# Attention scores as two extra columns per head of the feature weights, in the set-up of a graph-attention kernel

## The chip, the cores and the metric

The kernel runs on one core of a Trainium2 chip. The metric is device time in microseconds, the median of the runs of one program. A core has a matrix engine (TensorE, PE in the profile; its weight loads are PEld), VectorE (DVE), ScalarE (ACT), GpSimd (POOL) and SyncE (SP). Engines run their own instruction queues in order and wait for each other by semaphores. Sixteen DMA engines move data; here SP, POOL and at the very start ACT ask for transfers. Matmul results go to PSUM, 8 banks of 128 x 512 float32 values.

## The reference

Two layers over 4096 nodes with 512 features and a dense 4096 x 4096 adjacency matrix. Layer 0 is graph attention with 8 heads of 64 features, layer 1 an attention inside 32 graphs. The change concerns layer 0 alone, and of it the first three lines:

```python
feats = jnp.einsum('nf,hfo->hno', X, W)                  # 8 heads, 4096 x 64 each
s_self = jnp.einsum('hno,ho->hn', feats, a_self)         # one score per node and head
s_neigh = jnp.einsum('hno,ho->hn', feats, a_neigh)
dense = s_self[:, :, None] + s_neigh[:, None, :]
dense = jnp.where(dense > 0, dense, ALPHA * dense)       # ALPHA = 0.2
dense = dense * A[None, :, :]
attn = jax.nn.softmax(dense, axis=-1)
out = jnp.einsum('hij,hjo->hio', attn, feats) + b[:, None, :]
```

Then a relu, a residual and a layer norm; layer 1 follows on the result.

Because a score is feats times a vector, it is also X times (W a): one column of 512 weights per head and kind of score.

## The kernel before

**Set-up** (lines 601 to 822). The 4096 nodes are 32 tiles of 128, taken in 8 blocks k of 4 tiles u. For each block:

- `load_rows(k)` (L617) asks on SP for four tiles of x, into four buffers `xt_f`.
- `turn_rows(k)` transposes them on PE (L661), 16 transposes of 128 x 128, four to each of four PSUM tiles `ps_set`; ACT copies each PSUM tile to `xT_f` (L664) and sums it on the way.
- `scores(k)` multiplies xT by `wa`, the 16 columns W a (L672), one 32-row strip of PSUM for each of the four chunks c of the 512 features; ACT copies the strips to `st` (L680).
- `exponentials(k)` multiplies `st` by `stack`, which adds the four strips and turns the scores to columns (L686), and takes five exponentials on ACT (L695 to L700): `e_all`, `d_all` and `pu_j`. DVE then splits `e_all` into bf16 parts (L703 to L717).
- `features(k, u)` multiplies one tile by W (L743): four matmuls of 512 columns into one PSUM tile, and DVE adds b into `fb` (L751).
- `scaled_features(k, u)` makes `gst` = fb times an exponential (DVE, L757) and `fst`, the features split into two rounded parts (ACT L765, DVE L766); POOL stores both to DRAM as `g_d` and `f_d` (L778). `gst`, `fst` and `fb` have three buffers each.
- `rows_of_exponentials(k)` transposes `pu_j` on PE (L722), ACT copies it (L726), POOL stores it to `pu_d` (L730). `columns_of_exponentials(k)` transposes the copy back (L735) into `pu_all` (DVE, L736).

After blocks 3, 4 and 5 POOL also loads a first part of the adjacency matrix (L596). At the end column sums of the features are formed (L576, L583).

The weights' score columns come from DVE at the very start: four chunks times two kinds, a product (L647) and a reduction (L650).

All PSUM tiles of the set-up come from one pool of seven banks, in turn; the eighth bank is `ps_misc`, which the adjacency transposes (L1122) use later.

**After the set-up** come four passes over the adjacency matrix, one per pair of heads. The first turns adjacency tiles (PE L1122), casts them on ACT (L1126) and stores them (`at_d`, POOL L1127); all passes run the matmuls L1381, L1401 and L1415 over them, with the comparisons L1361 (DVE) and L1370 (ACT). Layer 1 (L961 to L1103) runs in the last pass and after it. SP loads `p_row` and `u_row` from `pu_d` for the passes (L1306, L1309).

**The order of the work.** PE's instructions run in the order in which the program is written (`manual_schedule` for PE, L455). The other engines' queues are ordered by a planner, which takes what it holds to be ready, earlier program lines first; on the chip each queue then runs strictly in that order.

## Time and profile before

| what | value |
|---|---|
| median of 3 runs | 2079.16 us (2077.47 to 2079.18) |
| span of the profiled execution | 2080.8 us |
| PE, DVE, ACT, POOL busy, share of the span | 98%, 80%, 74%, 12% |
| set-up: first L1122 transposes of the first pass start at | 162.90 us |
| set-up: features of the last tile end at | 161.83 us |
| one block of the set-up (L686 of one block to that of the next) | 18.47 us |
| L743, 256 records of 128x512 | 116.9 us busy |
| L672 and L686, 64 records each | 9.6 and 8.1 us busy |
| f_d stores, 32 of 512 KB each | 7.7 us to land, median |

A page of the profile gives shares over the whole span. A fp32 matmul appears as two records. Records of pipelined matmuls overlap, so their busy time is longer than the distance between them; the distances stand in the chain, which follows the work that ended last back from the end. In the timeline, the brackets name what an instruction waited for. The profiled execution has no time of its own beside its span; it lies 1.6 us above the median.

### The profile page before, as it was taken

What the parts mean: (1) busy time and instruction counts of PE and PEld (TensorE: products, weight loads), DVE (VectorE), ACT (ScalarE), POOL (GpSimd) and SP (SyncE); (2) the same over time, 40 slices, a digit from 0 to 9 for tenths busy, and PEclk for the clock granted to TensorE, in tenths of its full rate; (3) what the DMA queues carried; (4) which work ended last, traced back from release to release, by engine and by line L of the source; (5) the groups of instructions that cost most, each with busy time, mean ns of one, the idle gap of its engine ahead of it and who ended that gap; (6) DMA issues with size and microseconds to landing.
All of it is one profiled execution on the core that took longest, in us unless ns stands there. A gap on an engine that the chain in (4) does not pass through costs nothing.

```text
span 2080.8 us, 38068 instructions
## 1 busy us (share of the span) xinstructions
PE 2045.7 (98%) x14982; PEld 1005.3 (48%) x14982; DVE 1660.4 (80%) x2040; ACT 1536.7 (74%) x1821; POOL 246.4 (12%) x393
## 2 busy tenths in 40 slices
PE   8999999999999999999999999999999999999997
PEld 4555555454445544444445444444454444445443
DVE  5557887878799998798999999999975984886654
ACT  3338888888878989788899889998885666567420
POOL 2343222222100000000000000000200210210111
PEclk9999999999999999999999999999999999999999
DMA  8999999999899999888999999989974764775211
GB/s 249 267 257 247 270 292 259 296 260 285 261 326 342 347 346 337 275 303 285 323 317 334 310 344 331 330 288 363 321 242 138 247 250 129 227 272 167 72 48 43
DMA packets 207881, 551.28 MB, mean 265 GB/s; under 512 B 25292, under 2 KB 66252, under 8 KB 207692
## 3 DMA queue, kind: packets, MB, share of 16 engines
q1 hardware_dynamic: 140748, 425.79, 59.0%
q0 software_dynamic: 62784, 121.91, 23.3%
q8 instruction: 120, 1.97, 0.4%
q10 hardware_dynamic: 4160, 1.05, 0.2%
q14 instruction: 69, 0.57, 0.1%
HBM read 491.79 MB, written 107.22 MB: 288 GB/s over the span
## 4 chain that ended last, share of the span: by engine, by line
PE 83%; DMA 7%; issue 4%; DVE 2%; ACT 2%; POOL 1%; SPq 0%; POOLq 0%; ACTq 0%; DVEq 0%
PE acc L1401 36%; PE accf L1381 20%; PE ps_set L743 5%; PE ps_m L1059 5%; DMA at_d<-at 5%; PE ps_m L987 5%; PE dens L1415 5%; PE ps_m L1014 1%; PE ps_m L1073 1%; ACT mark L1370 1%; DVE q L1361 1%; PE ps_m L1122 1%; PE ps_m L916 1%; DMA f_s<-f_d 1%; DMA hs_d<-hst 1%
## 5 line engine op out<-in xcount | busy, mean ns | idle before, releaser
L1361 DVE SCALAR_TENSOR_TENSOR q<-p_row,d_all,at 128x1024 f32<-128x1024 f32 x1024 | 1242.0, 1278 | 171.4 <-PE acc L1401 143.7
L1370 ACT ACTIVATE mark<-q,nb_all 128x1024 fp8e4<-128x1024 f32 x896 | 994.6, 1145 | 176.1 <-DVE q L1361 160.3
L1401 PE MATMUL acc<-q,g_s 128*32 128x512 f32 x8192 | 903.0, 593 | 1.1 <-DVE q L1361 0.4
L1401 PEld LDWEIGHTS acc<-q,g_s 128*32 128x32 f32 x8192 | 264.5, 110 | 594.1 <-issue 533.1
L1381 PE MATMUL accf<-at,f_s 128*128 128x512 f32 x2048 | 494.5, 397 | 2.3 <-issue 1.8
L1381 PEld LDWEIGHTS accf<-at,f_s 128*128 128x128 f32 x2048 | 379.9, 189 | 111.7 <-issue 29.1
L1141 ACT ACTIVATE ck<-ck,neg_half_f 128x1024 f32<-128x1024 f32 x128 | 146.0, 1140 | 20.5 <-DMA ck<-in_adj_dram 20.5
L1142 ACT ACTIVATE ck<-ck,neg_quarter 128x1024 f32<-128x1024 f32 x128 | 146.3, 1143 | 1.8
L1126 ACT CAST at<-ps_m 128x1024 fp32r<-128x1024 fp8e4 x128 | 120.2, 1025 | 12.3 <-issue 5.9
L1415 PE MATMUL dens<-mark,e_b 128*6 128x512 fp8e4 x2048 | 125.4, 379 | 2.7 <-ACT mark L1370 2.7
L743 PE MATMUL ps_set<-w_sb_f,xT_f 128*128 128x512 f32 x256 | 116.9, 605 | 0.1
L987 PE MATMUL ps_m<-x1T,M_sb 128*128 128x512 f32 x256 | 113.1, 595 | 1.6 <-ACT x1T L968 1.6
L1059 PE MATMUL ps_m<-wvT,x1T 128*128 128x512 f32 x256 | 114.2, 594 | 0.0
L1246 POOL DMA_DIRECT2D hs_d<-hst x12 | 10.7, 895 | 832.9 <-DVE hst L1236 739.0
L1366 DVE TENSOR_SCALAR mark<-q,d_all 128x1024 fp8e4<-128x1024 f32 x128 | 95.7, 748 | 4.8
L1415 PEld LDWEIGHTS <-e_b 128*6 128x6 bf16 x2048 | 52.7, 86 | 83.0 <-issue 38.8
L1127 POOL DMA_DIRECT2D at_d<-at x128 | 68.8, 538 | 178.0 <-ACT at L1126 111.0
L765 ACT ACTIVATE fst<-fb 128x512 fp32r<-128x512 f32 x32 | 20.3, 636 | 85.3 <-DVE fb L751 48.3
L987 PEld LDWEIGHTS ps_m<-x1T,M_sb 128*128 128x128 f32 x256 | 47.9, 190 | 63.1 <-issue 60.1
L1059 PEld LDWEIGHTS ps_m<-wvT,x1T 128*128 128x128 f32 x256 | 47.6, 190 | 57.2 <-issue 56.0
L743 PEld LDWEIGHTS ps_set<-w_sb_f,xT_f 128*128 128x128 f32 x256 | 49.0, 199 | 51.3 <-issue 49.9
L994 ACT ACTIVATE zT<-ps_m,zb 128x512 f32<-128x512 f32 x32 | 21.8, 683 | 70.3 <-PE ps_m L987 70.3
(185 smaller groups left out, 1119.2 us busy)
## 6 DMA issues: line engine op xcount, KB each, us to landing
at<-at_d SPq DMA_DIRECT2D x384, 512.0 KB, 6.0
ck<-in_adj_dram SPq DMA_DIRECT2D x128, 512.0 KB, 5.5
f_s<-f_d SPq DMA_DIRECT2D x128, 512.0 KB, 7.4
at_d<-at POOLq DMA_DIRECT2D x128, 512.0 KB, 14.8
g_s<-g_d SPq DMA_DIRECT2D x128, 256.0 KB, 5.6
f_d<-fst POOLq DMA_DIRECT2D x32, 512.0 KB, 7.7
p_row<-pu_d SPq DMA_DIRECT2D x32, 512.0 KB, 6.7
a_b<-in_adj_dram POOLq DMA_DIRECT2D x32, 512.0 KB, 16.8
```

The costliest lines, as they stand in the source:

```text
L743: nc.tensor.matmul(pf, tile_j(xTs[k][:, c].rearrange("p u n -> p (u n)"), u), w_sb[:, c, :], start=(c == 0), stop=(c == FC - 1),)
L987: nc.tensor.matmul(pz, L1["M"][:, f, ts(c, P)], x1T[:, f, :], start=(f == 0), stop=(f == FC - 1),)
L1059: nc.tensor.matmul(pv, x1T[:, f, ts(u, P)], L1["wvT"][:, f, :], start=(f == 0), stop=(f == FC - 1),)
L1126: nc.scalar.copy(at, both[:, :, k])
L1141: tc.keep_in_program_order(nc.scalar.activation(ck, ck, AF.Square, bias=neg_half))
L1142: nc.scalar.activation(ck, ck, AF.Abs, bias=neg_quarter, accum_out=binp[:, k : k + 1])
L1361: nc.vector.scalar_tensor_tensor(q, p_row[h], d_j, ats[r, c, j].bitcast(F32), op0=OP.max, op1=OP.mult)
L1366: nc.vector.tensor_scalar(mark, q, d_j, None, op0=OP.is_gt, saturate=False)
L1370: nc.scalar.activation(mark, q, AF.Sigmoid, bias=nb_all[:, j, hh : hh + 1], scale=BIG, saturate=False,)
L1381: nc.tensor.matmul(accf[:, s, :], f_s[j // 4][:, j % 4, w, :], ats[r, c, j][:, ts(s, HB)], start=(j == 0 and w == 0), stop=(j == NT - 1 an ...
L1401: nc.tensor.matmul(acc[o : o + 32, s, :], g_s[j // 4][:, j % 4, h, o % FH : o % FH + 32], qs[j, h][:, ts(s, HB)], start=(j == 0), stop=(j ...
L1415: nc.tensor.matmul(dens[lo : lo + 6, :], e_b[:, j, 2 * r + h, :], marks[j, h][:, ts(s, HB)], start=(j == 0), stop=(j == NT - 1),)
```

## The change

`wa`, `stack`, `scores` and the strip copies `st` go. The weights become 66 columns per head: 64 of W and two of W a, which DVE's reductions write into the same tile `w_sb`. A tile's features and scores come out of the same accumulation. 8 x 66 = 528 columns don't fit a PSUM bank, so each chunk is two matmuls of 264 columns into two banks, from a pool `ps_feat` with two such tiles; the other pool has three banks in place of seven. The scores of a tile are then multiplied by the factors of the exponents (`powers`, DVE) and exponentiated, tile by tile. In block 0 the features take 64 columns per head, and `first_scores` makes the scores of its four tiles with matmuls of 16 columns. The order within a block changes: the turning of the next block stands behind features (k, 0) in every block, rows and columns of the exponentials are formed one block later, and in the last block behind the loop. `fb` moves to the pool of `q` (six buffers), `prod` to that of `gst`.

```diff
-    ) as xtp, tc.tile_pool(name="ps_setup", bufs=7, space=PSUM) as pss:
+    ) as xtp, tc.tile_pool(name="ps_setup", bufs=3, space=PSUM) as pss, tc.tile_pool(
+        name="ps_feat", bufs=2, space=PSUM
+    ) as psf:
...
+        FW = FH + 2
+        w_sb = one.tile([P, FC, H, FW], F32, name="w_sb_f")
...
-        wa = one.tile([P, FC, 32], F32, name="wa")
-        nc.vector.memset(wa, 0.0)
         for c in range(FC):
             for k in range(2):
-                prod = three.tile([P, H, FH], F32, name="fb")
...
+                prod = three.tile([P, H, FH], F32, name="gst")
+                nc.vector.tensor_mul(prod, w_sb[:, c, :, :FH], a_b2[:, k])
+                nc.vector.tensor_reduce(w_sb[:, c, :, FH + k], prod, AX.X, OP.add)
+        powers = one.tile([P, 5, H], F32, name="powers")
+        for i, v in enumerate((ALPHA, 1.0, ALPHA - 1.0, 1.0 - ALPHA, -ALPHA)):
+            nc.vector.memset(powers[:, i, :], v)
...
                 if u == 0:
-                    pts[c] = pss.tile([P, 4, P], F32, name="ps_set")
+                    last = k == 0 and c == FC - 1
+                    pts[c] = misc([P, 4, P]) if last else pss.tile([P, 4, P], F32, name="ps_set")
...
-        def scores(k):
...
-        def exponentials(k):
...
+        def exponentials(k, u, sc):
+
+            j = 4 * k + u
+            if u == 0:
+                pu_js[k] = two.tile([P, 4, 2, H], F32, name="pu_j")
+            st = small.tile([P, 5, H], F32, name="st")
+            for lo, hi, w in ((0, 3, 1), (3, 5, 0)):
+                nc.vector.tensor_tensor(
+                    st[:, lo:hi].rearrange("p k (q h) -> p k q h", q=2),
+                    sc[:, None, :, :, w].to_broadcast([P, hi - lo, 2, H // 2]),
+                    powers[:, lo:hi].rearrange("p k (q h) -> p k q h", q=2),
+                    OP.mult,
+                )
+            nc.scalar.activation(e_all[:, j], st[:, 0:2], AF.Exp)
+            nc.scalar.activation(pu_js[k][:, u], st[:, 3:5], AF.Exp)
+            nc.scalar.activation(d_all[:, j, :], st[:, 2], AF.Exp)
...
         def features(k, u):
-            pf = pss.tile([P, H * FH], F32, name="ps_set")
+            pf = psf.tile([P, 2, HB], F32, name="ps_fe")
+            pf = pf[:, :, : H * FW // 2].rearrange("p q (h w) -> p q h w", w=FW)
+            cols = slice(0, FW if k else FH)
             for c in range(FC):
...
+                for q in range(2):
+                    nc.tensor.matmul(
+                        pf[:, q, :, cols],
+                        tile_j(xTs[k][:, c].rearrange("p u n -> p (u n)"), u),
+                        w_sb[:, c, 4 * q : 4 * q + 4, cols],
+                        start=(c == 0),
+                        stop=(c == FC - 1),
+                    )
+            fb = qp.tile([P, C], F32, name="q")[:, : H * FH]
...
+            if k:
+                exponentials(k, u, pf[:, :, :, FH:])
             return fb
+
+        def first_scores():
+
+            ps = pss.tile([P, 4, H, 2], F32, name="ps_set")
+            for u in range(4):
+                for c in range(FC):
+                    nc.tensor.matmul(
+                        ps[:, u],
+                        tile_j(xTs[0][:, c].rearrange("p u n -> p (u n)"), u),
+                        w_sb[:, c, :, FH:],
+                        start=(u == 0 and c == 0),
+                        stop=(c == FC - 1),
+                        skip_group_check=True,
+                    )
+            for u in range(4):
+                exponentials(0, u, ps[:, u].rearrange("p (q h) w -> p q h w", q=2))
...
         for k in range(NB):
             if k + 1 < NB:
                 load_rows(k + 1)
...
+            fbs = {}
+            for u in range(4):
+                fbs[u] = features(k, u)
+                if u == 0 and k + 1 < NB:
+                    turn_rows(k + 1)
+                if u == 1 and k:
+                    rows_of_exponentials(k - 1)
+                if u == 2 and k:
+                    columns_of_exponentials(k - 1)
+                if u == 2 and k == 0:
+                    first_scores()
+                    for v in range(3):
+                        scaled_features(k, v, fbs[v])
+                if k or u == 3:
+                    scaled_features(k, u, fbs[u])
...
+            parts_of_exponentials(k)
             if k in (3, 4, 5):
                 tc.keep_in_program_order(load_adjacency(0, 4 * (k - 3)))
+        rows_of_exponentials(NB - 1)
         pS = pss.tile([P, PR], F32, name="ps_set")
         sums_to_columns(pS, S_part)
...
```

`parts_of_exponentials(k)` holds the splitting into bf16 parts that stood at the end of `exponentials(k)`; the partial column sums (L804 to L812) now stand behind features (7, 0) and (7, 1). The last `columns_of_exponentials` stays where it was, behind the column sums.

## The prediction

> **What bounds the kernel now.** I read the page first (share of each engine, the chain), then a table by stage, then the chain inside the set-up, then its waits.
>
> ```profile
> span 2080.8 us, 38068 instructions
> PE 2045.7 (98%) x14982; PEld 1005.3 (48%) x14982; DVE 1660.4 (80%) x2040; ACT 1536.7 (74%) x1821; POOL 246.4 (12%) x393
> PE 83%; DMA 7%; issue 4%; DVE 2%; ACT 2%; POOL 1%; SPq 0%; POOLq 0%; ACTq 0%; DVEq 0%
> ```
>
> TensorE carries 83% of the chain. The change touches the set-up only, so the stage table decides (columns: stretch, length, busy us and count of PE, PEld, DVE, ACT, POOL, clock, DMA share, GB/s).
>
> ```profile
> 0.00:20.00 20.00, 14.17 (x38) 6.81 (x38) 10.82 (x31) 3.70 (x9) 0.81 (x10) 1.00 0.84 249
> 80.00:100.00 20.00, 20.00 (x80) 10.26 (x79) 10.95 (x27) 6.41 (x20) 8.07 (x11) 1.00 0.86 247
> 120.00:140.00 20.00, 20.00 (x80) 9.99 (x82) 11.01 (x28) 6.28 (x20) 8.97 (x12) 1.00 1.05 220
> 163.00:168.60 5.60, 2.46 (x32) 2.09 (x32) 4.42 (x7) 5.05 (x7) 3.63 (x6) 0.83 0.58 203
> ```
>
> From 20 to 163 us PE has no idle time; DVE and ACT are about half and a third busy; DMA is near full from 95 us on. One block of four tiles, as the chain shows it (start, length, what):
>
> ```profile
> 74.53 0.84 PE ps_set L686 x8
> 75.37 1.79 PE ps_set L661 x16
> 77.17 3.44 PE ps_set L743 x8
> 80.61 0.35 PE ps_set L735 x4
> 80.95 3.64 PE ps_set L743 x8
> 84.59 1.00 PE ps_set L672 x8
> 85.59 0.54 PE ps_set L722 x4
> 86.12 6.88 PE ps_set L743 x16
> 93.00 0.84 PE ps_set L686 x8
> ```
>
> The period is 93.00 - 74.53 = 18.47 us, all PE: 13.96 features, 1.79 transposes of x, 0.54 + 0.35 transposes of the exponentials, and 1.84 for what the change removes (L672 1.00, L686 0.84).
>
> Last, waits that cost PE nothing yet, and the end of the set-up:
>
> ```profile
> 112.27 0.69 DVE L757 TENSOR_TENSOR gst<-fb,e_all 128x512 f32<-128x512 f32 x1 [3.50 <-DMA g_d<-gst]
> 113.73 0.63 ACT L765 ACTIVATE fst<-fb 128x512 fp32r<-128x512 f32 x1 [8.23 <-DMA f_d<-fst]
> 114.65 0.63 ACT L664 ACTIVATE xT_f<-ps_set 128x512 f32<-128x512 f32 x1
> 162.90 1.33 PE L1122 MATMUL ps_m<-ident_b,a_b 128*128 128x128 bf16 x16
> 168.64 9.85 PE L1381 MATMUL accf<-at,f_s 128*128 128x512 f32 x32
> ```
>
> ACT stands at fst (L765) until an earlier f_d store lands, and behind it in ACT's queue stand the copies of the turned rows (L664). PE runs on only because seven PSUM tiles let it.
>
> **The change part by part** (against the profiled execution; its span of 2080.8 is 1.6 us, 0.08%, above the median 2079.16 of the runs, so I subtract the shift from the median).
>
> *Features.* Each fp32 matmul is two records. A 512-column record takes 3.43/8 = 0.429 us (L743, L1059), a 128-column one 0.112 (L661: 1.79/16; L1014: 3.57/32), both with a 128x128 weight load hidden. A line through both gives 0.224 us at 264 columns. A tile becomes 16 such records, 3.59 us, against 3.44: four tiles cost 0.61 more. Bounds: 0.220 (pure streaming at the slope 0.827 ns per column plus 2 ns) to 0.231 (adding the 17 ns by which L1381's 512-column single-pass record, 7.38/32 = 0.231, exceeds half of 0.429): 0.4 to 1.0 per block. The Trainium skill (Perfetto Trace Analysis, Matmuls) says larger matmuls are more efficient than smaller ones, which speaks against the split; by the two rows above that is 3 ns per record (0.2176 on the line at 256 columns against 0.429/2), inside the 0.61; the page gives no figure of its own for the sum.
>
> *Scores and stacking removed.* 1.00 + 0.84 off PE per block; also ACT's st copy (0.57) and a DVE memset and reduction (0.17, 0.25), both in the shade of PE. New period: 4 x 3.59 + 0.2 for changes of kind (13.96 - 8 x 4 x 0.429) + 1.79 + 0.54 + 0.35 = 17.23, so 1.23 less.
>
> *Exponentials per tile.* Per block eight small DVE products (nearest: L703, 0.18) and twelve exps (L695: 0.20, every 0.08) in place of five. At most 1.5 and 2.4 us on engines that have 9 and 13 us of every 20 free: nothing while PE is the limit. Chain per tile on DVE and ACT: 0.69 (fb) + 0.3 + 0.3 (exps) + 0.69 (gst) + 0.69 (stt) = 2.7 us, under the 3.6 of a tile, so two feature buffers suffice as long as no store is late.
>
> *Block 0.* Features (0,0) end at 14.75 as before. Next in PE's order is now the turning of block 1, whose rows are requested at 10.59 and land at about 18.2 (the DMA rate falls to nothing there); before, it ran at 21.79 and didn't wait. From 18.2: turning 1.97, features (0,1), (0,2) 7.05, first scores (32 records at 0.105, the rate of L686, 3.45), features (0,3) 3.6, features (1,0) 3.6: turning of block 2 at 37.9, against 38.44. But PE stands idle for 3.4 us. In the trace, after 3.04 idle us at the end of the set-up (1.82 + 1.22), the next 32 accf matmuls took 9.61 us instead of 7.38: the window's clock is 0.83 for that reason. So between 0 and 2.2 us for a cold clock; the idle stretch is like that row and I take 2.2: +1.7 in all. The skill (TensorE: Matmul & The Clock Gate, What's actually happening) has half rate after an idle window of some 3.4 us and full rate after as much work; by that page an estimate of 1.7 us in place of 2.2, and a sum of -0.9 in place of the -0.4 below.
> The product-and-reduce pairs now write into w_sb beside what features (0,u) read. If that were tracked by whole tiles, features (0,0) would end near 21.6, and block 2 be turned 1 us later than I take; but DVE already interleaves writes and reads of different elements of e_b (L710 twice before L711), so I leave that at 0.
>
> *Blocks 1 to 6.* From the turning of block 2 to the end of features (7,0): 148.40 - 38.44 = 109.96 before, 6 x 17.23 = 103.4 after: -6.6.
>
> *Block 7.* 161.83 - 148.40 = 13.43 before; 3 x 3.59 + 0.25 + 0.54 + 0.35 + 1.0 (partial sums) = 12.9 after: -0.5.
>
> *The tail.* rows_of_exponentials moves from before features (k,3) to one block later, for the last block behind everything. What moves: 4 transposes, an ACT copy (0.61), a POOL store pu_d (0.53 of issue), which passes the g_d and f_d stores of the next tiles on POOL; on SP the p_row and u_row loads (55.23, 56.10) wait a block longer, with the x rows behind them, which are needed only a block after they are asked for: nothing. But after the last features PE now waits for fb 0.8, products 0.3, exps 0.3 to 0.9 (fst may stand first on ACT), then 0.54 transposes, 0.80 column sums beside the ACT copy, 0.35: 3.4 us to the first L1122, against 1.07: +2.3 (1.5 to 3.5). Behind it wait the adjacency casts on ACT, then accf. One fst (0.54) no longer stands between the first casts: -0.5.
>
> *PSUM.* The turning needs four tiles and has three (one bank each), so chunk 3 waits for ACT's copy of chunk 0. Transposing starts at 0; chunk 0 is ready at 0.65, copied at 1.25, released at about 1.4; chunk 3 would start at 1.35. If ACT is free: 0.1 per block, +0.6 (0 to 4.2, see rivals).
>
> *Late stores.* With three banks ACT's wait reaches PE. Features (4,3) end at 108.03, so its fst was ready at 108.9 and ran 4.8 late. After, the first adjacency load and all behind it move up by 4.4 us, the features by 5: late by 5.3. Chunk 3 is released fst 0.55, copy 0.6 and 0.15 after that start, 7.5 us after features (4,3), and is due after 3.59 + 1.35 = 4.95: 2.6 us of PE idle. The later late stores (131.20, 148.12: 3.8 and 2.3 late) then fall under the 2.7 that is tolerated. Bounds: 0 (covered) to 5 (each of them felt): +2.6.
>
> Sum: +1.7 - 6.6 - 0.5 + 2.3 - 0.5 + 0.6 + 2.6 = -0.4 us. After the set-up PE is the limit, and the shift passes through: 2079.16 - 0.4 = 2078.8. I call 0.2% (4.2 us) the least that a measurement of this kernel tells from no change; this lies inside.
>
> **The rivals.**
> *A, the saving comes through (24%).* No cold clock, and the late stores stay hidden: -0.4 - 2.2 - 2.6 = -5.2, 2074.0. For it: no idle of 1.34 us at 19.5 slowed PE, and DMA share is only 0.65 and 0.50 in the last 10 us of the set-up, so stores are not the limit overall. Against it: the two rows used above.
> *B, ACT takes the exponentials before the first copy (22%); slower.* The exps of tile (k,0) need fb and two products, ready 1.15 us after its features. If ACT's order has them ahead of the copy of chunk 0, that ends near 2.0, chunk 3 starts at 2.1: 0.7 per block, 4.2 instead of 0.6; and in block 5 the exps wait for a DVE that waits for the late fst: 2 more. -0.4 + 3.6 + 2.0 = +5.2: 2084.4. It decides from a first copy that starts later than 0.75 us after the transposes. For it: today the exps do stand ahead of the copies (93.88 to 94.36). Against: there they are ready first, and fst, ready early, was put after the copies, so the order follows readiness, and chunk 0 is ready 0.5 us sooner.
> *C, the first pass falls behind (8%).* From 300 to 500 us the chain runs over at_d stores and adjacency loads, with 27.3 us per eight tiles against 25.8 before. Another 1.5 in each of four groups gives +6: 2084.8. Against: the DMA share of 0.50 at 160 us says that the set-up's stores have drained.
>
> **How the numbers follow.** The sum has 46%, with its own range of 2075.5 to 2082.5 (front 0 to 2.2, stores 0 to 5, split 0.4 to 1.0 not all at one end). Faster: four fifths of A, since 5.2 is little over 4.2, and a rest of the sum, 0.25. Slower: most of B, C and a rest, 0.31. Same 0.44. The range takes in A and B, 2073 to 2085.5.
>
> **What would show it.** Records of L743's successor 0.224 us apart; a period of 17.2 to 17.4 in blocks 2 and 3; PE waiting on x rows at 14.8 to 18.2 and slow records after; one PE wait of 2 to 3 us in the turning of block 6 behind xT's copy; 3.4 us from the last features to L1122. I'm wrong if the copies stand behind the exps, if 264-column records cost over 0.231, or if pass 0 changes its period.

## The result, and the profile after

The changed kernel takes 2083.80 us (median of 21 runs; the kernel before beside them on the same chip 2080.04, also 21). The ratio is 1.0017, with a 95% interval of 1.0010 to 1.0023: about 3.5 us slower (3.8 by the two medians). The forecast was 2078.8, a shift of -0.4, and "no change that can be told" as the likeliest outcome; the measured shift is the other way. An effect of this size is below the 0.2% that the prediction called measurable; 21 runs a side told it all the same.

The profiled execution after has a span of 2081.7 us and a time of its own of 2084.0, so 2.3 us lie outside the span. In the other profiled executions shown below it is 1.9 to 2.6, and in every execution on record of the kernel before, run beside the experiments, 2.6 or 2.7. If that held for the profiled execution of before as well, its span of 2080.8 stood for some 2083, some 3 us above the median. This is why the two spans differ by only 0.9 us. Stages are therefore compared by the traces below, totals by the medians.

The page after, its span, engines, the chain by engine, and the feature matmuls:

```profile
span 2081.7 us, 38500 instructions
PE 2042.6 (98%) x15142; PEld 1055.3 (51%) x15142; DVE 1666.8 (80%) x2107; ACT 1541.4 (74%) x1869; POOL 247.2 (12%) x393
PE 83%; DMA 7%; issue 4%; ACT 3%; DVE 2%; POOL 1%; POOLq 0%; DVEq 0%; ACTq 0%; SPq 0%
L724 PE MATMUL ps_fe<-w_sb_f,xT_f 128*128 128x264 f32 (+1 forms) x512 | 121.9, 395 | 0.3
```

Nothing on this page shows what happened. The stage table does (columns as before: stretch, length, busy us and count of PE, PEld, DVE, ACT, POOL, clock, DMA share, GB/s):

```profile
0.00:20.00 20.00, 11.61 (x43) 8.46 (x44) 11.08 (x35) 4.62 (x12) 0.81 (x10) 0.95 0.84 249
80.00:100.00 20.00, 20.00 (x105) 17.21 (x104) 13.02 (x38) 8.11 (x30) 8.97 (x13) 1.00 0.89 282
100.00:120.00 20.00, 19.03 (x98) 15.88 (x97) 10.97 (x33) 6.57 (x25) 7.24 (x10) 1.00 1.08 267
120.00:140.00 20.00, 14.39 (x69) 12.40 (x70) 8.71 (x27) 4.29 (x18) 5.43 (x7) 0.91 0.98 232
```

Before, PE was busy for all 20 us from 120 to 140, and now it is for 14.39, with the DMA engines about as busy as before (0.98 against 1.05). In the first row it loses 2.6 us as well.

The chain after, through one block that runs freely, and then through the place where the set-up stalls (start, length, what):

```profile
57.91 1.87 PE ps_set L655 x16
59.78 3.57 PE ps_fe L724 x16
63.35 0.44 PE ps_set L700 x4
63.79 3.57 PE ps_fe L724 x16
67.36 0.35 PE ps_set L713 x4
67.70 7.33 PE ps_fe L724 x32
75.03 1.87 PE ps_set L655 x16
...
112.65 0.91 POOL a_b L588
...
118.40 14.45 DMA f_d<-fst
132.96 0.63 ACT fst L769
134.53 1.11 PE ps_set L655 x4
135.64 4.48 PE ps_fe L724 x16
```

A block takes 75.03 - 57.91 = 17.12 us, and a tile's sixteen records 3.57: the new period and the new record are there as predicted. Then one store, asked for at 118.40, takes 14.45 us to land where the median over all f_d stores is 6.6. ACT waits for it before it may write `fst`; the copies of the turned rows stand behind `fst`; PE's transposes wait for the copies. In the timeline (brackets: idle before, and what ended it):

```profile
18.41 3.04 PE L655 MATMUL ps_set<-ident_f,xt_f 128*128 128x128 f32 x13 [0.23 <-DMA xt_f<-in_x_dram]
109.51 0.64 ACT L769 ACTIVATE fst<-q 128x512 fp32r<-128x512 f32 x1 [6.16 <-DMA f_d<-fst]
111.08 0.66 PE L655 MATMUL ps_set<-ident_f,xt_f 128*128 128x128 f32 x4 [0.51 <-ACT xT_f L658]
132.96 0.63 ACT L769 ACTIVATE fst<-q 128x512 fp32r<-128x512 f32 x1 [8.64 <-DMA f_d<-fst]
133.81 0.57 ACT L658 ACTIVATE xT_f<-ps_set 128x512 f32<-128x512 f32 x1
134.53 1.11 PE L655 MATMUL ps_set<-ident_f,xt_f 128*128 128x128 f32 x4 [5.61 <-ACT xT_f L658]
167.73 1.58 PE L1124 MATMUL ps_m<-ident_b,a_b 128*128 128x128 bf16 x16
```

PE waits 0.51 us in the turning of block 6, where the prediction had its 2.6, and 5.61 in that of block 7, where it had none; after that wait its four transposes take 1.11 in place of 0.66, and the next tile 4.48 in place of 3.57. The first pass starts at 167.73, against 162.90 before.

### The profile page after: what moved, and what is told of

Same layout as the page of the kernel before. It is cut to its first block, busy times and chain, and to the rows that moved or that the text cites. A ratio compares the mean times of both kernels' runs of the same rounds, so it can differ in the third digit from the quotient of the medians.

```text
span 2081.7 us, 38500 instructions
## 1 busy us (share of the span) xinstructions
PE 2042.6 (98%) x15142; PEld 1055.3 (51%) x15142; DVE 1666.8 (80%) x2107; ACT 1541.4 (74%) x1869; POOL 247.2 (12%) x393
## 3 DMA queue, kind: packets, MB, share of 16 engines
q10 hardware_dynamic: 4160, 1.05, 0.2%
## 4 chain that ended last, share of the span: by engine, by line
PE 83%; DMA 7%; issue 4%; ACT 3%; DVE 2%; POOL 1%; POOLq 0%; DVEq 0%; ACTq 0%; SPq 0%
PE acc L1403 37%; PE accf L1383 20%; PE ps_m L1061 5%; PE dens L1417 5%; PE ps_m L989 5%; PE ps_fe L724 3%; DMA at_d<-at 3%; ACT mark L1372 2%; PE ps_m L1016 1%; PE ps_m L1075 1%; DVE q L1363 1%; PE ps_m L1124 1%; DMA f_d<-fst 1%; PE ps_m L918 1%; DMA a_b<-in_adj_dram 1%
## 5 line engine op out<-in xcount | busy, mean ns | idle before, releaser
L724 PE MATMUL ps_fe<-w_sb_f,xT_f 128*128 128x264 f32 (+1 forms) x512 | 121.9, 395 | 0.3
L724 PEld LDWEIGHTS ps_fe<-w_sb_f,xT_f 128*128 128x128 f32 x512 | 101.1, 202 | 14.9 <-issue 1.4
L1069 DVE TENSOR_TENSOR v_t<-ps_m,bv_row 128x512 f32<-128x512 f32 x32 | 21.9, 686 | 61.7 <-PE ps_m L1061 61.7
```

Source lines behind the costliest of these rows:

```text
L724: nc.tensor.matmul(pf[:, q, :, cols], tile_j(xTs[k][:, c].rearrange("p u n -> p (u n)"), u), w_sb[:, c, 4 * q : 4 * q + 4, cols], start=(c ...
```

## The experiments

Two questions were open: what makes the stores late, and how much of a shift of the set-up reaches the total. "First product" below is the start of the first adjacency transposes, the end of the set-up. Before it is at 162.90, after at 167.73. Differences in total are to the kernel before, run beside on the same chip.

First products come from one profiled execution each, and block 0 is not the same in all of them. In the runs that leave the changed kernel's block 0 alone, the turning of block 2 starts at 39.48 to 42.15 us in the timeline: 40.63 (after), 42.15 (four buffers), 41.04 (loads early), 39.48 (loads late), 40.74 (traffic), 39.55 (stores on SP). The granted clock makes the difference (last section). Differences of one or two microseconds between first products can come from this alone.

### More room for the late stores: four buffers for fst

```diff
-    ) as two, tc.tile_pool(name="setup3", bufs=3, side="right") as three, tc.tile_pool(
+    ) as two, tc.tile_pool(name="setup3", bufs=3, side="right") as three, tc.tile_pool(name="setup4", bufs=4, side="right") as fstp, tc.tile_pool(
...
-            fst = three.tile([P, PR, 2, FP], F32R, name="fst")
+            fst = fstp.tile([P, PR, 2, FP], F32R, name="fst")
```

> Edit on the changed kernel: fst gets four buffers in place of three, nothing else. Theory S (late f_d stores, reaching PE through the three PSUM banks of the turning): ACT waits for f_d shrink by about one tile period, 4 us each, so the PE waits in the turning of blocks 6 and 7 (0.5 and 5.6 us, and about 1.6 us of cold records behind the second) fall to 0 to 2.5 us, and the first pass begins at 160 to 163 us instead of 167.8. Rival S2 (the turning waits for another cause, such as the DVE queue): the start stays within 1 us of 167.8. Of the total, if a shift of the set-up passes through: 2076 to 2079, 5 to 8 us under the changed kernel, 1 to 4 under the kernel before. If pass 0 takes shifts up (its middle follows the adjacency transfers): within 2 us of the changed kernel.

Measured: 2080.66 us, ratio 0.9997 (0.9988 to 1.0007); first product 165.12, later than the 160 to 163 of the theory. No `fst` waits for a store any longer, but the lateness shows up in the next two places, DVE's `gst` and PE's rows of x:

```profile
132.79 0.69 DVE L761 TENSOR_TENSOR gst<-q,e_all 128x512 f32<-128x512 f32 x1 [6.23 <-DMA g_d<-gst]
130.44 1.77 PE L655 MATMUL ps_set<-ident_f,xt_f 128*128 128x128 f32 x13 [1.12 <-DMA xt_f<-in_x_dram]
137.11 0.60 PE L700 MATMUL ps_set<-ident_f,pu_j 128*16 128x128 f32 x4 [1.33 <-ACT xT_f L658]
```

So the wait of `fst` was the price (2.6 us of the set-up, though block 0 came 1.5 later here, and about 3.5 of the total), but not the cause: stores and loads alike are late in this stretch.

### The turning of block 1 one tile later

```diff
-                if u == 0 and k + 1 < NB:
+                if u == (k == 0) and k + 1 < NB:
                     turn_rows(k + 1)
```

> Edit on the changed kernel: in block 0 the rows of block 1 are turned behind features (0,1) instead of features (0,0). Theory F (the front loses by waiting for the x rows and by the cold clock after it): the wait of 2 to 4 us between 14 and 18.4 us vanishes, the turning of block 2 begins 2 to 5 us before the 40.8 of the changed kernel. Rival F2 (the wait only moves: ACT's copies of the turned rows now stand behind fst of tile (0,0), which waits for DVE until 21 us): less than 1.5 us earlier. Total, if shifts pass through: 2 to 5 us under the changed kernel by F, less than 1.5 by F2.

Measured: 2082.43 us, ratio 1.0004 (0.9996 to 1.0013); turning of block 2 at 40.79, as in the changed kernel; first product 168.10. The wait for rows of x is gone, and another has taken its place:

```profile
22.53 1.08 PE L655 MATMUL ps_set<-ident_f,xt_f 128*128 128x128 f32 x4 [2.60 <-ACT xT_f L658]
```

In ACT's queue the planner had put the `fst` of tile (0,0) ahead of the copies, and that one waits for DVE until 21.27, as rival F2 had it. A step moved in PE's order alone moved nothing.

The same, with ACT's order mended (the `fst` of block 0 held in program order, behind the score work):

```diff
-            nc.scalar.activation(fst[:, :, 0, :], fr, AF.Copy, scale=-1.0)
+            high = nc.scalar.activation(fst[:, :, 0, :], fr, AF.Copy, scale=-1.0)
+            if k == 0:
+                tc.keep_in_program_order(high)
```

> The changed kernel with block 1's transposes behind the second tile's features, and the copies of block 0's scaled features held behind the score work of that block, so that they cannot stand ahead of the copies of the turned rows. If the 2.4 us by which the turning of block 2 falls late (40.79 against 38.44) come from TensorE's wait for rows of x at 14.3 to 18.4 us and its cold clock after it: that wait becomes under 1.5 us, and the turning of block 2 starts at 36.5 to 38.5. If only the wait goes and the clock stays low in the first 25 us: 38.5 to 40.5. In the total the late stores of blocks 4 to 6 take the gain back (an earlier TensorE only waits longer for them): first product at 166.5 to 168, total within 2 us of the changed kernel. If the front's delay passes through on its own: first product at 165 to 166, total -1.5 to -3 us.

Measured: 2082.53 us, ratio 1.0003 (0.9994 to 1.0012). The turning of block 2 begins at 35.26 in the timeline, 5.4 us earlier than in the changed kernel and earlier than expected; 1.4 of this is a clock that did not fall behind the first scores (last section). It meets the late stores all the same (waits of 6.76, 3.08 and 8.17 us at 106, 119 and 129 us), and the first product is at 164.45: of 5.4 us gained in front 3.3 are left at the end of the set-up. The late stores themselves landed earlier too: the `fst` of tile (5,3) ran at 128.57, 4.4 us before the 132.96 of the changed kernel. The expectation that the stores would take all of it back was too strong.

### A pure shift: eight more matmuls at the end of the set-up of the kernel before

```diff
+        for u in range(2):
+            pf = pss.tile([P, H * FH], F32, name="ps_set")
+            for c in range(FC):
+                nc.tensor.matmul(
+                    pf,
+                    tile_j(xTs[NB - 1][:, c].rearrange("p u n -> p (u n)"), u),
+                    w_sb[:, c, :],
+                    start=(c == 0),
+                    stop=(c == FC - 1),
+                )
         pS = pss.tile([P, PR], F32, name="ps_set")
```

> Edit on the kernel before: two feature products too many at the end of the set-up, eight matmuls of 512 columns whose result nobody reads, 6.9 us of PE by their rows. Theory T1 (a shift of the set-up's end passes through): total 6 to 7.5 us over the kernel before. Rival T2 (pass 0 is held in its middle by the adjacency transfers, which take a shift up, as the two profiles suggest, +4.6 us at 262 us and +0.4 at 528): 0 to 3 us over it, and the lag in the profile is gone by 530 us.

Measured: 2084.63 us, ratio 1.0020 (1.0010 to 1.0031). The first product moves from 162.90 to 170.00, accf from 168.64 to 175.25 (6.6 us), the total by 4.2: about 60% passes, not all of it. This lies between the two theories. In the trace the groups of dens lag by 6 us up to 410 us and by about 4 from 460 on; how much of that step belongs to the execution of before is asked below.

### Rows and columns of the exponentials a block later, in the kernel before

```diff
-                columns_of_exponentials(k - 1)
+                rows_of_exponentials(k - 1)
...
+            if k:
+                columns_of_exponentials(k - 1)
             scaled_features(k, 2, fbs[2])
...
-            rows_of_exponentials(k)
+            if k == NB - 1:
+                rows_of_exponentials(k)
```

> Edit on the kernel before: rows and columns of the exponentials one block later, as in the changed kernel; the seven PSUM banks and all else stay. Theory R (the loads of p_row, which must wait for these rows, fall onto the second adjacency load and make the f_d stores behind it later): the p_row load of chunk 1 moves from 91.7 to about 110 us, and fst of tile (5,3) waits until 133 to 136 us instead of 131.2; PE feels it only if the wait exceeds what seven banks hide, so the total is within 2 us of the kernel before. Rival R2 (the p_row loads don't matter): fst of tile (5,3) within 1 us of 131.2, the total the same.

Measured: 2079.79 us, ratio 0.9996 (0.9987 to 1.0004): no change. The `fst` wait that ends at 113.73 in the kernel before ends at 109.55 here, where the changed kernel has 109.51, and the one that ends at 131.20 ends at 131.19:

```profile
109.55 0.63 ACT L765 ACTIVATE fst<-fb 128x512 fp32r<-128x512 f32 x1 [5.18 <-DMA f_d<-fst]
```

So the first late store landed 4.2 us earlier by this move alone, at the old pace of PE. The moved loads are not what makes the second one late, and their place costs nothing, as predicted.

### The adjacency loads earlier

The first suspect was the three loads that POOL asks for after blocks 3, 4 and 5. First they were moved ahead, in both kernels:

```diff
-            if k in (3, 4, 5):
-                tc.keep_in_program_order(load_adjacency(0, 4 * (k - 3)))
+            if k in (0, 1, 2):
+                tc.keep_in_program_order(load_adjacency(0, 4 * k))
```

> The changed kernel with its three adjacency loads for the first pass asked for after blocks 0, 1 and 2 of the set-up, in place of blocks 3, 4 and 5; nothing else moves. Theory T (the scaled features' stores are late because the block's loads and stores already fill the DMA engines in blocks 4 to 6, and the adjacency loads lie on top of them there): with the loads gone from that stretch the waits of the copies fst on the stores (6.2 us at 109.5, 8.6 us at 133.0) fall to under 1 us, TensorE does not wait in the turnings of blocks 6 and 7, and the first product of the first pass starts at 159 to 161 us in place of 167.7. In the total 60 to 100% of that, -4 to -8 us: 2076 to 2080. Rival R (the stores are late because they are asked for late, behind the loads of columns and rows on their queue): the waits stay, total unchanged within 1.5 us. Rival M (the loads only move their trouble to blocks 1 to 3, where rows of x come late): TensorE waits for rows of x in blocks 2 to 4 for 3 to 8 us, and the total stays or rises.

> The same move of the adjacency loads in the kernel before: the control. Theory T: there seven banks of PSUM let TensorE run ahead of the late stores, so it gains nothing from earlier stores: the first product of the first pass at 162.9 +-1, total within 2 us of the kernel before (2078.5 to 2082.5). If the kernel before gained as much as the changed one (5 us or more), the loads cost both kernels the same, and would not be what sets the two apart.

Measured: the changed kernel 2089.61 us, ratio 1.0041 (1.0027 to 1.0054), first product 174.44; the kernel before 2087.79, ratio 1.0030 (1.0017 to 1.0042), first product 171.84. The rival that moves the trouble had it right, and for both kernels, against the expectation of the control. Of the changed kernel:

```profile
81.95 0.66 PE L655 MATMUL ps_set<-ident_f,xt_f 128*128 128x128 f32 x4 [3.53 <-ACT xT_f L658]
100.41 1.20 PE L655 MATMUL ps_set<-ident_f,xt_f 128*128 128x128 f32 x9 [1.10 <-DMA xt_f<-in_x_dram]
106.17 1.12 PE L655 MATMUL ps_set<-ident_f,xt_f 128*128 128x128 f32 x4 [4.56 <-ACT xT_f L658]
```

and of the kernel before:

```profile
78.41 0.33 PE L661 MATMUL ps_set<-ident_f,xt_f 128*128 128x128 f32 x1 [1.64 <-DMA xt_f<-in_x_dram]
81.33 0.47 PE L661 MATMUL ps_set<-ident_f,xt_f 128*128 128x128 f32 x1 [2.59 <-DMA xt_f<-in_x_dram]
```

Where the loads were put, the stall is. Seven banks cover a late store, but not late rows of x.

### The adjacency loads later

```diff
-            if k in (3, 4, 5):
-                tc.keep_in_program_order(load_adjacency(0, 4 * (k - 3)))
+            if k in (5, 6, 7):
+                tc.keep_in_program_order(load_adjacency(0, 4 * (k - 5)))
```

> The changed kernel with its three adjacency loads asked for after blocks 5, 6 and 7 in place of 3, 4 and 5; nothing else moves. Theory T (a block's own loads and stores nearly fill the DMA engines, and whatever is laid on top of them makes the scaled features' stores late): the waits of fst on the stores at 109 and 133 us fall below 1.5 us each, TensorE does not wait in the turnings of blocks 6 and 7, the first product of the first pass starts at 159.5 to 163 in place of 167.7, and the total falls by 2 to 6 us (2078 to 2082), if the loads, now asked for at some 128 to 165 us, still land before the first pass needs each (the second part of the pass at about 190 us, the third at about 215). Rival L (the pass then waits for its loads): TensorE waits for a_b in the first 60 us of the pass, and the total rises by 3 us or more. Rival R (the stores are late for a reason of their own queue): the waits of fst stay.

> The same move in the kernel before, whose seven banks of PSUM cover the late stores: set-up unchanged (first product at 162.9 +-0.7), total within 2 us of the kernel before if the loads still land in time; +3 us or more if the first pass waits for them (rival L).

Measured for the changed kernel: 2078.79 us, ratio 0.9989 (0.9980 to 0.9997), first product 158.26, 9.5 us earlier, and earlier than expected. Of these, 1.1 stand in block 0, ahead of anything that the edit moves, and 8.3 behind it. Its chain and its stage table:

```profile
108.11 1.87 PE ps_set L655 x16
109.98 3.57 PE ps_fe L724 x16
...
125.22 1.87 PE ps_set L655 x16
127.09 3.57 PE ps_fe L724 x16
```

```profile
100.00:120.00 20.00, 20.00 (x104) 17.05 (x104) 12.94 (x38) 7.61 (x29) 6.73 (x10) 1.00 0.97 270
120.00:140.00 20.00, 20.00 (x103) 17.31 (x102) 12.84 (x38) 7.21 (x26) 8.95 (x12) 1.00 1.01 237
```

No `fst` waits for a store; PE is busy throughout, and the blocks keep 17.11 us to the end. In the kernel before the same move gives 2085.06, ratio 1.0021 (1.0012 to 1.0029). Its set-up is nearly unmoved (first product 163.44, expected 162.2 to 163.6), but its blocks still take 18.47 us, the third load is asked for only at 167.40, and the first pass waits, as its rival had it:

```profile
181.25 1.55 PE L1122 MATMUL ps_m<-ident_b,a_b 128*128 128x128 bf16 x16 [3.46 <-DMA a_b<-in_adj_dram]
```

So the change gains where the loads stand late, and loses where they were. With the loads late in both, the changed kernel is 6.3 us ahead (2078.79 against 2085.06), of which 4.1 are what the kernel before loses by the move.

### Five banks in the kernel before

```diff
-    ) as xtp, tc.tile_pool(name="ps_setup", bufs=7, space=PSUM) as pss:
+    ) as xtp, tc.tile_pool(name="ps_setup", bufs=5, space=PSUM) as pss:
```

> The kernel before with five banks of PSUM for its set-up in place of seven. Theory T (the same late stores, which seven banks cover): the stores of block 5 land where they did (131 to 133 us), and TensorE now waits for the copies of the turned rows behind fst in the turnings of blocks 5 to 7, in sum 3 to 8 us; the first product at 166 to 171 us in place of 162.9; total +2 to +6 us. Rival (the banks do not matter, the lateness comes with the changed order of the exponentials alone): no such wait, first product at 162.9 +-1.0, total within 1.5 us of the kernel before.

Measured: 2086.64 us, ratio 1.0029 (1.0018 to 1.0040); first product 165.72, just under what was expected. From its timeline:

```profile
114.65 0.63 ACT L765 ACTIVATE fst<-fb 128x512 fp32r<-128x512 f32 x1 [7.97 <-DMA f_d<-fst]
115.77 0.66 PE L661 MATMUL ps_set<-ident_f,xt_f 128*128 128x128 f32 x4 [0.91 <-ACT pu_j L700]
116.66 3.71 PE L743 MATMUL ps_set<-w_sb_f,xT_f 128*128 128x512 f32 x8 [0.24 <-DVE fb L751]
132.78 0.63 ACT L765 ACTIVATE fst<-fb 128x512 fp32r<-128x512 f32 x1 [6.01 <-DMA f_d<-fst]
180.72 3.07 PE L1381 MATMUL accf<-at,f_s 128*128 128x512 f32 x8 [1.99 <-DMA at_d<-at]
```

The store of block 5 lands about where it did, and with two banks fewer ACT's wait reaches PE. But PE loses only some 1.2 us to it, in the turning of block 6 alone. The wait at 132.78 costs nothing, because PE, at 18.5 us a block, comes to that turning only at 133.45. The other half of the first product's 2.8 us, and what the total has lost beyond them, come from elsewhere (rows of x in the turning of block 4, 0.87, and a wait of 1.99 in the first pass). The banks are part of the explanation. That the faster PE, which arrives earlier at the same store, is the larger part is what is left over; no run changes the pace of PE alone.

### By the engines' work, or by the queue?

The adjacency loads and the stores are asked for by POOL, on one queue. Two runs tell the two mechanisms apart: the loads late, with copies of the same values put back in their old places on ACT's queue,

```diff
+    idle_d = dram.tile([3, C, 4 * P], F32, name="idle_d")
...
+            if k in (3, 4, 5):
+                tc.keep_in_program_order(
+                    nc.scalar.dma_start(idle_d[k - 3], adj[:C, (k - 3) * 4 * P : (k - 2) * 4 * P])
+                )
             if k in (5, 6, 7):
                 tc.keep_in_program_order(load_adjacency(0, 4 * (k - 5)))
```

> The changed kernel with the adjacency loads late (after blocks 5, 6 and 7), and at their old places, after blocks 3, 4 and 5, three copies of the same 1024 x 512 float32 values of the adjacency matrix from DRAM to DRAM, asked for by ScalarE on a queue of its own, which nothing reads. The copies only add traffic; nothing waits for them. Theory W (the work that the DMA engines have in blocks 4 to 6 is what makes the stores late): the waits of fst on the stores come back, 3 us or more each in blocks 4 and 5, TensorE waits 3 to 9 us in the turnings of blocks 6 and 7, the first product of the first pass starts at 162 to 170 us in place of 158.3, total +2 to +6 us over the kernel with late loads (2081 to 2085). Theory Q (the stores stand behind an adjacency load in the one queue that GpSimd feeds): copies on another queue don't hold them up, no wait of fst over 1.5 us, first product at 157.5 to 160, total within 2 us of 2078.8.

and the loads in their old places, with the f_d stores on SP's queue.

```diff
-                nc.gpsimd.dma_start(dst[:, k, :, ts(u, n)].rearrange("r p n -> p r n"), src)
+                q = nc.gpsimd if dst is g_d else nc.sync
+                q.dma_start(dst[:, k, :, ts(u, n)].rearrange("r p n -> p r n"), src)
```

> The changed kernel, adjacency loads where they were (after blocks 3, 4 and 5), but the stores f_d asked for by SyncE's queue in place of GpSimd's; the stores g_d stay. Theory Q: the f_d stores no longer stand behind the adjacency loads, the waits of fst on them fall under 1.5 us, first product at 157.5 to 161 (unless gst then waits for g_d). Theory W: the waits stay, in sum 8 us or more, and the first product starts at 164 to 169. In either case rows of x stand behind stores in SyncE's queue, and TensorE may wait for them in any block; that part is told by what it waits for, and the total says nothing of the theories alone.

Measured: with the traffic 2093.57 us, ratio 1.0060 (1.0046 to 1.0073), first product 175.48; with the stores on SP 2087.51, ratio 1.0035 (1.0022 to 1.0049), first product 169.12. The waits of the first (line, what it waited for: us in total, times, longest):

```profile
PE ps_set L656 <- DMA xt_f<-in_x_dram: 16.0, 11, 3.7
ACT fst L770 <- DMA f_d<-fst: 10.8, 2, 6.2
```

and of the second:

```profile
ACT fst L769 <- DMA f_d<-fst: 28.6, 6, 6.9
PE ps_set L655 <- DMA xt_f<-in_x_dram: 10.4, 10, 3.9
```

Traffic that shares no queue with the stores brings the waits back, and stores that share no queue with the loads keep theirs. Between 85 and 180 us the copies raised the median landing of the f_d stores from 6.6 to 10.6 us and that of the rows of x from 8.4 to 13.8, against the run with late loads alone; the stores that changed queue landed in 7.3, where on POOL's queue they took 7.1. It is the work asked of the DMA engines, not the order in one queue, that makes the stores late. Whether the engines themselves or the memory behind them set the pace, these runs do not separate. In the second run the stores share a queue with the rows of x, which that run alone would leave open; the first run has no such sharing. In the first run more of the delay fell on the rows of x, on SP's queue, than expected, and the loss was larger: 175 us where 162 to 170 were expected. Those copies also write four times what a load writes into `a_b` (2048 KB against 512 KB).

The Trainium skill (DMA: Bandwidth & Descriptors, Queues, rings and completion order) says that a DMA engine serves the queues it has work for in turn, packet by packet. The two runs agree with that: copies on ACT's queue held up both POOL's stores and SP's loads. The packets themselves no run shows.

### A version that beats both

The three cures that don't touch the loads together (four buffers for `fst`, the turning of block 1 with ACT's order held, and the last rows of exponentials behind the column sums), without and with the late loads:

```diff
-        rows_of_exponentials(NB - 1)
         pS = pss.tile([P, PR], F32, name="ps_set")
         sums_to_columns(pS, S_part)
+        rows_of_exponentials(NB - 1)
```

> The changed kernel with three edits at once: block 1's transposes behind the second tile's features with the copies of block 0's features held behind its score work, four buffers for fst, and the sums over columns ahead of the last rows of exponentials. The adjacency loads stay after blocks 3, 4 and 5. Four buffers alone brought the first product to 165.1 and the turning alone to 164.5; if each keeps its own part: 161 to 163. If both only run up against the same full DMA engines in blocks 4 to 6: 163 to 165. Total 2078 to 2081: same as the kernel before.

> The kernel with the three edits, and the adjacency loads after blocks 5, 6 and 7 as well. Theory T: the set-up runs at TensorE's own pace, the first product starts at 154 to 158, and the total is 2073 to 2078 (faster than the kernel before by 0.1 to 0.3%). Rival L (the first pass waits for the late loads, or its own stores and loads set its pace): the first product early, but the groups of dens no earlier than in the kernel before from 300 us on, total 2079 to 2084.

Measured: 2077.28 us, ratio 0.9982 (0.9973 to 0.9991), first product 161.54; and with the late loads 2075.71, ratio 0.9973 (0.9964 to 0.9982), first product 154.91:

```profile
154.91 1.20 PE L1126 MATMUL ps_m<-ident_b,a_b 128*128 128x128 bf16 x16
170.10 1.07 PE L1126 MATMUL ps_m<-ident_b,a_b 128*128 128x128 bf16 x16 [1.29 <-DMA a_b<-in_adj_dram]
```

That is 5.3 us less than the kernel before, with the change in it. The first product moved by 8.0 us; 1.29 of it is paid again where the second load is now waited for. Between these two runs the late loads are not the only difference: block 0, the same program in both, ended 3.6 us later in the first (turning of block 2 at 38.82 against 35.26), again by the clock. The kernel before was not run with these cures, except for the late loads, so how much of the 5.3 us is the change's own is not shown.

### How much of a shift passes

| kernel | first product, us | to before | total to before, us | ratio (95%) |
|---|---|---|---|---|
| before + eight matmuls | 170.00 | +7.1 | +4.2 | 1.0010 to 1.0031 |
| before, rows late | 162.36 | -0.5 | -0.7 | 0.9987 to 1.0004 |
| before, loads early | 171.84 | +8.9 | +7.2 | 1.0017 to 1.0042 |
| before, five banks (a wait of 1.99 in the pass) | 165.72 | +2.8 | +6.1 | 1.0018 to 1.0040 |
| before, loads late (a wait of 3.46 in the pass) | 163.44 | +0.5 | +4.1 | 1.0012 to 1.0029 |
| after | 167.73 | +4.8 | +3.8 | 1.0010 to 1.0023 |
| after, four buffers | 165.12 | +2.2 | +0.2 | 0.9988 to 1.0007 |
| after, turning later | 168.10 | +5.2 | +2.0 | 0.9996 to 1.0013 |
| after, turning held | 164.45 | +1.6 | +2.0 | 0.9994 to 1.0012 |
| after, three cures | 161.54 | -1.4 | -3.7 | 0.9973 to 0.9991 |
| after, loads late | 158.26 | -4.6 | -2.2 | 0.9980 to 0.9997 |
| after, both | 154.91 | -8.0 | -5.3 | 0.9964 to 0.9982 |
| after, loads early | 174.44 | +11.5 | +9.1 | 1.0027 to 1.0054 |
| after, stores on SP | 169.12 | +6.2 | +6.0 | 1.0022 to 1.0049 |
| after, late loads and copies | 175.48 | +12.6 | +12.1 | 1.0046 to 1.0073 |

The total is the difference of two medians of runs made together; the first product is that of one execution, whose own time lies up to 3.7 us from the median of its kernel (four buffers: 2084.34 against 2080.66). Read from end to end, without the two rows with the long waits in the pass, 20.6 us of first product made 17.4 us of total, some eight tenths; single rows with a shift of 4 us or more pass four to ten tenths.

Whether anything of a shift is absorbed is not settled. Held against the profiled execution of before, the lag of the groups of dens changes in two places, from 404 to 434 us and from 514 to 543: from 4.5 to 2.3 to 0.4 us for the changed kernel, from 6.3 to 4.4 to 4.1 for the eight matmuls. But the version with the three cures, which is early, gains there as well (from -2.4 to -3.6 to -5.7), and so does the kernel before with its rows late, whose set-up has hardly moved (from -0.4 to -2.1 and then -1.3). So a part of these steps is time that the execution of before lost there, which was, by the estimate above, itself some 3 us over its median.

## Why the prediction was wrong

By its own terms, in us of the set-up:

| term | predicted | measured |
|---|---|---|
| record of 264 columns | 0.224 | 3.57/16 = 0.223 |
| new period | 17.23 | 17.12 |
| Block 0 | +1.7 | 40.79 - 38.44 = +2.35 |
| Blocks 1 to 7, without stores, with PSUM | -7.1 + 0.6 = -6.5 | -7.8 (late loads) |
| the tail up to the first product | +2.3 | 167.73 - 164.68 - 1.07 = +2.0 |
| the tail from there to accf | -0.5 | (173.07 - 167.73) - (168.64 - 162.90) = -0.4 |
| **Late stores** | **+2.6, at most 5** | **+8.3** |
| total for 4.4 at accf | all of it | +3.8 |

The -7.8 is from the run with late loads, in which no store is late: 155.22 - 39.65 = 115.57 from the turning of block 2 to the end of the features, against 161.83 - 38.44 = 123.39 before. The +8.3 is what is then left of the 4.83 us by which the first product came later: 4.83 - 2.35 + 7.8 - 2.0. The trace after has 7.9 of it in its lines: waits of 0.51, 0.46 and 5.61, and 0.45 and 0.91 by which the slow records behind the last one were longer.

**Late stores is the step that failed.** The mechanism was right: ACT waits for a store, the copies stand behind it, and three banks pass the wait to PE. Its size was wrong, for two reasons.

It let the landings move up with PE ("the first adjacency load and all behind it move up by 4.4 us, the features by 5"). That load was asked for at 93.26, 0.3 us earlier than before (93.59). The first late `fst`, of tile (4,3), did run 4.2 us earlier (109.51 against 113.73), but by the later place of the exponentials' rows: with that move alone it ran at 109.55 in the kernel before. The features of that tile ended at 105.5, only 2.5 us earlier. So the wait in the turning of block 6, where the term had put its 2.6, was 0.51 and a rest of 0.46.

And it said of the next late store that it would "fall under the 2.7 that is tolerated". Before, that store, of (5,0), was asked for at 119.13, and the `fst` of (5,3), which waits for it, ran at 131.20:

```profile
119.13 0.76 POOL L778 DMA_DIRECT2D f_d<-fst  x1 [1.33 <-DVE fst L766]
131.20 0.63 ACT L765 ACTIVATE fst<-fb 128x512 fp32r<-128x512 f32 x1 [5.15 <-DMA f_d<-fst]
```

After, it was asked for at 118.40, 0.7 us earlier, and the `fst` ran at 132.96, 1.8 us later. The turning of block 7 began at 127.45 where it had begun at 130.62, so 5.4 us before the store landed, and PE stood for 5.61 us and then ran slow (four transposes 1.11, the next tile 4.48).

The profile before had a sign of it: a DMA share of 1.06 and 1.05 between 100 and 140 us. The prediction read it as "near full" and took only the single store's lateness from it. The rows of the page give the sum: a block writes four f_d stores of 512 KB and four g_d stores of 256 KB and loads four tiles of 256 KB, 4.2 MB. In 18.47 us that is 227 GB/s and in 17.12 us 245, where the windows near a share of 1 moved 220 to 326. An adjacency load comes on top; the same values as float32 are 2 MB. A block of 17.11 us can have its own bytes, as the run with late loads shows; with a load on top, in blocks 4 and 5, its stores came late. In that run blocks 6 and 7 have a load on top (asked for at 125.61 and 142.72) and no late store; but there no rows of x are loaded any more, 1 MB less per block.

**The shift passes through** was the smaller miss, in the direction that hid part of the other: 4.4 us later at accf made 3.8 in total, and 6.6 made 4.2 with the eight matmuls.

**Block 0** came 0.65 short, and less well than this looks. The rows of x came at the predicted time (the last thirteen transposes start at 18.41, 18.2 was forecast). The cold clock was taken at 2.2; measured, after 3.09 us of waits in sum, thirteen transposes took 3.04 us in place of 1.77, 1.3 us more. The estimate of 1.7 from the Trainium skill (TensorE: Matmul & The Clock Gate, What's actually happening) was the nearer. What made up for it was not foreseen: the first scores took 3.93 for 3.45, and behind them the clock fell a second time, with PE busy throughout; the next two tiles took 8.66 in the timeline, where with the turning held, at full clock, they took 7.27 (after, then turning held):

```profile
32.13 8.66 PE L724 MATMUL ps_fe<-w_sb_f,xT_f 128*128 128x256 f32 x32
28.15 7.27 PE L724 MATMUL ps_fe<-w_sb_f,xT_f 128*128 128x256 f32 x32
```

**Features, Scores and stacking, Exponentials per tile, the tail** came out within 0.3 us each. **PSUM** (0.1 per block) is not refuted: in the blocks without late stores the timeline shows no wait at chunk 3, yet a turning takes 1.87 in place of 1.79, by a cause that no run shows.

Three small slips of the working change nothing: 32 records at 0.105 are 3.36 and not 3.45; 0.224 and 17 ns are 0.241 and not 0.231, far above the 0.223 measured either way; and before, PE did stand idle for some 1.6 us between 20 and 25 us.

Rival **A** (the saving comes through, -5.2) has its condition, no late store, in the run with late loads: there accf starts at 163.50, 5.1 us before the 168.64 of the kernel before, and the total falls by 2.2. Rival **B** did not occur: in the turnings without a late store ACT takes the copy of chunk 0 first and the exponentials after it. Behind the first late `fst` its second half shows: the exponentials of tile (5,0) wait 3.69 us for DVE, until 114.72, ahead of the copies of chunks 1 to 3, and from there comes the rest of 0.46. Rival **C** did not occur in the changed kernel: its lag in the first pass is 4.6 us at 193 us and 4.5 at 404. The first pass waits for its loads only where they were moved late (3.46 us in the kernel before, 1.29 with the three cures as well, 0.38 in the changed kernel). None of the three signs by which the prediction said that it would be wrong is what failed it.

## What to carry to other kernels

Before a stage is shortened, add up what it asks of the DMA engines and divide by the new, shorter time. Where this comes near the rate that the busy engines moved in the profile, the saving can end at the next late store, wherever PE then happens to stand, and a smaller PSUM pool passes that wait on. A share near 1 alone does not settle it: with the loads late it stood at 0.97 and 1.01, and no store was late. Nor does a landing simply follow the work that asks for it: here the store was asked for 0.7 us earlier and landed 1.8 later, and where the front of the set-up moved up by 5.4 us it landed 4.4 earlier. Look then for bulk loads in the stage that are needed only later; to move them out of it was worth more here than a fourth buffer (first product 158.26 against 165.12), as long as the next stage doesn't wait for them.

## What the runs showed of the hardware

- The same transposes, after the same kind of wait for rows of x, ran at half rate in some executions and not in others: after waits of 3.09 us in sum (after) and 3.16 (loads early, traffic) thirteen took 3.03 or 3.04 us, after 2.26 (loads late) and 2.47 (stores on SP) 1.77 and 1.76. The program up to there is the same, so less than a microsecond of idle time, or chance, decided over 1.3 us of PE.
- The granted clock also fell without any idle time of PE. Behind the first scores, 32 records of 16 columns in some 4 us, it was 0.50 from 32 to 34 us and 0.75 from 34 to 36 (after), and the 32 records of two tiles took 8.66 us. They took 10.24 with four buffers and 9.94 with the three cures, where the clock stayed at 0.50 for longer, and 7.27 with the turning held and with the three cures and late loads, where it stayed at 1.00. What decides is not shown.
- A DMA share of about 1 was measured at quite different rates, from 220 GB/s (before, 120 to 140 us) to 326 (before, 60 to 80): the share tells that the engines are busy, the rate does not.
- Matmuls that write 264 columns cost 0.223 us a record, as the line through 128 and 512 columns had it. Those of block 0 write 256 columns in four runs of 64, leaving out two of every 66, and cost no more: 6.91/32 = 0.216, where the line gives 0.2176.
